# VectorE's attention and router operations in program order, an earlier bias copy, and a kept output product

## Chip, core and metric

The kernel runs on one core of one Trainium2 chip. The metric is the device time of one execution in microseconds (us). Engines: TensorE (PE; its weight loads are listed as PEld), VectorE (DVE), ScalarE (ACT), GpSimd (POOL), SyncE (SP, which only issues DMAs here).

## The reference, cut to what matters

Two layers on x of shape (2, 2048, 256), float32. Layer 0 is a gated linear attention plus a quantised linear layer. Layer 1, which the change touches, is softmax attention plus a mixture of experts chosen by a Sinkhorn router:

```python
xn = _layernorm(x, axis=-1)
# attention: 16 heads of 16; the first 8 look back, the last 8 ahead (ALiBi bias)
scores = jnp.einsum('bhqd,bhkd->bhqk', q, k) * (1.0 / np.sqrt(hd)) + bias[None]
attn = jax.nn.softmax(scores, axis=-1)
out = jnp.einsum('bhqk,bhkd->bhqd', attn, v)
...
return out @ Wf + bf
# router: 20 Sinkhorn iterations on 4096 tokens x 8 experts, two experts for each token
for _ in range(n_iters):
    la = la - jax.scipy.special.logsumexp(la, axis=-1, keepdims=True)
    la = la - jax.scipy.special.logsumexp(la, axis=-2, keepdims=True)
...
_, top_idx = jax.lax.top_k(pi, TOP_K)
...
x = x + _L1_attn_ref(...) + _L1_ffn_ref(...)
```

## The kernel before

The program has three stages in time: layer 0 (to about 437 us), attention with the router in the background (437 to 997 us), and the experts (997 us to the end).

A scheduler in the tile framework sets the order of instructions on each engine. It may bring an instruction forward past others of its engine, as its own estimate of the times says. `tc.keep_in_program_order` pins one instruction: pinned instructions keep the order among themselves in which the program writes them.

**Attention** (`attention`, L1613) goes over tiles: per batch b (2), per direction way (2) and per 256 queries qt (8), so 32 tiles. Way 0 goes from the shortest to the longest tile; way 1 then starts with the shortest again. A tile is cut into units of up to 512 columns for each of four rows of heads. In the main loop each unit does the following:
- `scores` (L1741): products sc into PSUM on PE (L1748), exponentials pt on ACT (L1754).
- `keep_only` (L1759): the first two units of a tile lie on the diagonal; VectorE masks their pt with keepmask (L1766), one unit after their scores.
- `add_up` (L1804): two units later (LATE = 2), the weighted sums o_ps on PE (L1779). The one PSUM buffer of o_ps is used by all tiles, so the first sums of a tile wait until VectorE has copied the last tile's to o_sb (L1812).
- one chore: a finished tile leaves a generator `normalise` (L1696), which does one step in each unit: transposes o_tr (L1705), inv and on on VectorE (L1708, L1712); and for the second tile of a pair also transposes on_tr and the copy onT (L1723, L1725), and two output products f_ps, each added to acc on VectorE (L1731, L1736). After way 1 a DMA writes the finished rows of acc (L1739).
- one step of the router's generator `background` (not in the second and third unit of a tile).

**The router** is `DirectSinkhorn` (L1505) and `Routing.steps` (L1927). Each of 20 iterations has two steps: row sums, their reciprocals and a scaling of pi (L1538, L1516, L1517), column sums sk_c (L1541); then a product sk_ps with a matrix of ones on PE (L1544) and the scaling by columns (L1516 to L1547). Then come ranks (L1949 to L1961), weights (L1966, L1970), the product place_ps (L1978, L1979), upto, place (L1982 on), and the rows of the weights' table. `decide` (L1652) tests whether a general program must run, with the product d_ps (L1675). Once the router is done, POOL scatters the rows to a table (L2089), 64 DMAs, two for each 128 tokens.

**The values' bias**, `value_bias` (L1633), is called at a quarter of the units, which is where batch 0 changes its direction: VectorE spreads bv to bvb (L1637, pinned), PE multiplies it with wf to b_ps (L1641), VectorE adds that to half_bias (L1644, L1645).

Pinned before are the copy bvb and, where an o_sb copy was issued since the last unit, the mask behind it; the other VectorE operations of attention and router are free. PSUM has, beside o_ps, seven buffers "mm" that sc, o_tr, on_tr, f_ps, sk_ps, b_ps, place_ps and d_ps share.

The experts' stage (`Experts`, L2210) multiplies blocks of up to 256 rows: x_ps (transposes of loaded rows xb), h_ps (L2179), y_ps (L2195), and adds the results to the output by indirect DMAs (L2204). Its first pieces also work off what chores are left.

Of the kernel before, what the change touches and what calls it, by code (L numbers as in the profile page):

```python
# [61 lines left out]
P = 128  # L62
# [37 lines left out]
VW = H1 * VC + HR - VC  # L100

# [152 lines left out]
def usual_way(ctx, tc, a, out, c, blocks):  # L254
# [25 lines left out]
    routing = Routing(nc, later, a, c)  # L280
    attention(tc, a, out, acc, la, norms, spans, c, operands, ready, routing, blocks)
# [3 lines left out]
def general_way(ctx, tc, a, out, c):  # L285
# [10 lines left out]
    routing = Routing(nc, later, a, c)  # L296
# [1208 lines left out]
class DirectSinkhorn:  # L1505


    def __init__(self, nc, pool, psum, la, pi, grown, ones_mat):
        self.nc, self.pool, self.psum, self.ones_mat = nc, pool, psum, ones_mat
        self.la, self.pi, self.grown = la, pi, grown  # L1510

    def scale(self, sums, axis):

        nc = self.nc
        by = self.pool.tile([P, sums.shape[1]], F32, tag=f"sk_by{axis}", name="sk_by")
        nc.vector.reciprocal(by, sums)  # L1516
        nc.vector.tensor_tensor(  # L1517
            self.pi, self.pi, by.unsqueeze(axis).to_broadcast([P, NT, NE]), ALU.mult
        )
        most = self.pool.tile([P, 1], F32, tag=f"sk_most{axis}", name="sk_most")  # L1520
        nc.vector.tensor_reduce(most, by, AX.X, ALU.max)
        return most

    def steps(self):


        nc, pool, pi = self.nc, self.pool, self.pi
        rmax = pool.tile([P, NT], F32, tag="sk_r", name="sk_r")
        nc.vector.tensor_reduce(rmax, self.la, AX.X, ALU.max)
        nc.vector.tensor_tensor(  # L1530
# [3 lines left out]
        nc.vector.memset(self.grown, 1.0)  # L1534
        yield
        for _ in range(SINKHORN_ITERS):
            rsum = pool.tile([P, NT], F32, tag="sk_r", name="sk_r")
            nc.vector.tensor_reduce(rsum, pi, AX.X, ALU.add)  # L1538
            most = self.scale(rsum, 2)
            csum = pool.tile([P, NE], F32, tag="sk_c", name="sk_c")  # L1540
            nc.vector.tensor_reduce(csum, pi.rearrange("p t e -> p e t"), AX.X, ALU.add)  # L1541
# [4 lines left out]
            nc.vector.tensor_scalar(most, most, cmost, 1.0, ALU.mult, ALU.max)  # L1546
            nc.vector.tensor_tensor(self.grown, self.grown, most, ALU.mult)  # L1547
# [65 lines left out]
def attention(ctx, tc, a, out, acc, la, norms, spans, c, operands, ready, routing, blocks):  # L1613
# [18 lines left out]

    def value_bias():  # L1633


        tc.keep_in_program_order(
            nc.vector.tensor_copy(ready.bvb, ready.bv.unsqueeze(2).to_broadcast([P, 2, P]))  # L1637
        )
        ps = ps_m.tile([P, E], F32, tag="mm", name="b_ps")
        for e in range(2):  # L1640
            nc.tensor.matmul(  # L1641
                ps, lhsT=ready.bvb[:, e, :], rhs=wf[:, e, :], start=e == 0, stop=e == 1
            )
        nc.vector.tensor_tensor(c.half_bias, c.half_bias, ps, ALU.add)  # L1644
        nc.vector.tensor_scalar(c.half_bias, c.half_bias, 0.5, None, ALU.mult)  # L1645

    def router():
        yield from DirectSinkhorn(nc, p2, ps_m, la, pi, grown, c.ones_mat).steps()
        yield from routing.steps(p2, ps_m, pi)
        yield from decide()  # L1650

    def decide():  # L1652

        high = p2.tile([P, 1], F32, tag="high", name="high")
        nc.vector.tensor_reduce(high, norms[:, 0, :], AX.X, ALU.max)
        least = p2.tile([P, 1], F32, tag="least", name="least")
        entry = p2.tile([P, NT, NE], F32, tag="sk_ex", name="entry")
        nc.vector.tensor_tensor(entry, routing.second, pi, ALU.mult)
        of_token = p2.tile([P, NT], F32, tag="sk_r", name="of_token")
        nc.vector.tensor_reduce(of_token, entry, AX.X, ALU.max)  # L1660
        nc.vector.tensor_reduce(least, of_token, AX.X, ALU.min)
        within = p2.tile([P, 1], F32, tag="within", name="within")
        nc.vector.tensor_scalar(within, least, TINY, None, ALU.is_ge)
        small = p2.tile([P, 1], F32, tag="small", name="small")
        nc.vector.tensor_scalar(small, grown, GROWTH, None, ALU.is_le)
        nc.vector.tensor_tensor(within, within, small, ALU.mult)
        inside = p2.tile([P, NSTRIP * HG * 8], F32, tag="sk_part", name="inside", bufs=1)
        nc.vector.tensor_scalar(
            inside, spans.rearrange("p s h n j -> p (s h n j)"), math.exp(-SPAN), None, ALU.is_ge
        )  # L1670
        nc.vector.tensor_reduce(small, inside, AX.X, ALU.min)
        nc.vector.tensor_tensor(within, within, small, ALU.mult)
# [7 lines left out]
        nc.vector.tensor_copy(row, ps)  # L1680
        both = p2.tile([1, P // 2], F32, tag="dboth", name="dboth")
        nc.vector.tensor_tensor(both, row[:, 0 : P // 2], row[:, P // 2 : P], ALU.mult)
        nc.vector.tensor_scalar(both, both, 0.98 * LIMIT**2, None, ALU.is_le)
        ok = p2.tile([1, 1], F32, tag="dok", name="dok")
        nc.vector.tensor_reduce(ok, both, AX.X, ALU.min)
        nc.vector.tensor_scalar(row[:, P : P + 1], row[:, P : P + 1], float(P), None, ALU.is_equal)
        nc.vector.tensor_tensor(ok, ok, row[:, P : P + 1], ALU.mult)
        nc.vector.tensor_scalar(ok, ok, -1.0, 1.0, ALU.mult, ALU.add)
        nc.vector.tensor_copy(c.general, ok)
        nc.vector.tensor_tensor(ok, ok, routing.over[:, 0:1], ALU.max)  # L1690
        nc.vector.tensor_copy(c.special, ok)
# [4 lines left out]
    def normalise(b, way, qt, o_sb):  # L1696
# [11 lines left out]
        nc.vector.reciprocal(inv, by_head[:, :, :, HD])  # L1708
        for n in range(2):

            at = (1 - n) * 64
            nc.vector.tensor_tensor(  # L1712
# [12 lines left out]
        nc.vector.tensor_copy(onT, ps.rearrange("p n t -> p (n t)"))  # L1725
        yield
        t0 = b * TPB + half * 4
        for n2 in range(2):
# [7 lines left out]
            nc.vector.tensor_tensor(acc[:, ts, :], acc[:, ts, :], ps, ALU.add)  # L1736
# [22 lines left out]
    def keep_only(way, pt, masked, pinned):  # L1759

# [5 lines left out]
        ins = nc.vector.tensor_tensor(  # L1766
# [3 lines left out]
        if pinned:  # L1770
            tc.keep_in_program_order(ins)
# [30 lines left out]
    o_ps, routed, unmasked, copied = None, False, None, False  # L1802

    def add_up():  # L1804
        nonlocal o_ps, copied
# [3 lines left out]
        weighted_sums(step, pieces, pt, o_ps, first, last)  # L1809
        if done:  # L1810
            o_sb = p2.tile([P, 2 * QT], F32, tag="o_sb", name="o_sb")
            nc.vector.tensor_copy(o_sb, o_ps)  # L1812
            copied = True
            chores.append(normalise(*step, o_sb))
            rest.append(True)
            b, way, qt = step
            if qt == (0 if way else N // QT - 1) and b + 1 < B:
                operands.load_values(b + 1, way, values[b, way])
                for g in range(2):
                    operands.load(b + 1, 2 * way + g)  # L1820

# [30 lines left out]
    at = 0  # L1852
    experts = Experts(tc, a, out, c, rooms, blocks)
    ahead = experts.todo[0:2]
    for n, (step, pieces, widths, masked, first, last, done) in enumerate(units):
        b, way, qt = step
        if n == len(units) // 4:
            value_bias()
# [8 lines left out]
        if unmasked:  # L1867
            keep_only(*unmasked, copied)
        unmasked, copied = (way, pt, masked) if masked is not None else None, False
        waiting.append((step, pieces, pt, first, last, done))  # L1870
        if len(waiting) > LATE:
            add_up()
        if rest:
            rest.pop()
        elif chores:
            if next(chores[0], True):
                chores.popleft()
# [8 lines left out]
    if unmasked:  # L1886
        keep_only(*unmasked, copied)
# [4 lines left out]
    for _ in experts.pieces(begun=True):  # L1892
        for _ in range(2):
            if chores and next(chores[0], True):
                chores.popleft()


class Routing:
# [3 lines left out]
    def __init__(self, nc, pool, a, c):  # L1902
        self.nc, self.a, self.c = nc, a, c
# [23 lines left out]
    def steps(self, pool, psum, pi):  # L1927
# [5 lines left out]
        nc = self.nc  # L1933
# [14 lines left out]
        for ts in (slice(0, NT // 2), slice(NT // 2, NT)):  # L1948
            nc.vector.tensor_tensor(beaten[:, ts], other[:, ts], mine[:, ts], ALU.is_gt)  # L1949
            yield  # L1950
            nc.vector.tensor_tensor(equal[:, ts], other[:, ts], mine[:, ts], ALU.is_equal)
            yield
            equal_f = equal[:, ts].rearrange("p t e j -> p t (e j)")
            nc.vector.tensor_tensor(
# [4 lines left out]
            nc.vector.tensor_tensor(beaten[:, ts], beaten[:, ts], equal[:, ts], ALU.add)  # L1959
            yield  # L1960
            nc.vector.tensor_reduce(rank[:, ts], beaten[:, ts], AX.X, ALU.add)  # L1961
            yield
        part = tile_("sk_part", [P, NT, NE], tag="sk_part")
        for r, mark, to in ((0, first, self.weights), (1, second, part)):
            nc.vector.tensor_scalar(mark, rank, float(r), None, ALU.is_equal)
            nc.vector.tensor_tensor(  # L1966
# [3 lines left out]
        nc.vector.tensor_tensor(self.weights, self.weights, part, ALU.add)  # L1970
# [3 lines left out]
        nc.vector.tensor_tensor(both, first, second, ALU.add)  # L1974
# [7 lines left out]
        nc.vector.tensor_copy(upto.rearrange("p t e -> p (t e)"), in_front[:, 1, :])  # L1982
        place = tile_("place", [P, NT, NE], tag="sk_part")
        nc.vector.tensor_tensor(
# [5 lines left out]
        while step < NT:  # L1990
            more = tile_(f"upto{step}", [P, NT, NE], tag="sk_ex")
            nc.vector.tensor_copy(more[:, 0:step, :], upto[:, 0:step, :])
            nc.vector.tensor_tensor(
# [7 lines left out]
        nc.vector.tensor_scalar(number, count, float(BS // 2 - 1), None, ALU.add)  # L2001
        nc.vector.tensor_scalar(number, number, BS.bit_length() - 1, None, ALU.logical_shift_right)
        blocks = tile_("blocks", [P, 2, NE])
        full, half = blocks[:, 0, :], blocks[:, 1, :]
        nc.vector.tensor_copy(full, number)
        in_full = tile_("in_full", [P, NE])
        nc.vector.tensor_scalar(in_full, full, float(BS), None, ALU.mult)
        nc.vector.tensor_tensor(half, count, in_full, ALU.is_gt)
        yield
        end = blocks  # L2010
        for step in (1, 2, 4):
            more = tile_(f"end{step}", [P, 2, NE])
            nc.vector.tensor_copy(more[:, :, 0:step], end[:, :, 0:step])
            nc.vector.tensor_tensor(
# [5 lines left out]
        nc.vector.tensor_tensor(start, end[:, 0, :], full, ALU.subtract)  # L2020
        nc.vector.tensor_scalar(start, start, float(BS), None, ALU.mult)

        away = tile_("away", [P, NE])
        nc.vector.tensor_tensor(away, end[:, 1, :], half, ALU.subtract)
        nc.vector.scalar_tensor_tensor(away, end[:, 0, :], -2.0, away, ALU.mult, ALU.add)
        nc.vector.tensor_scalar(
# [4 lines left out]
        nc.vector.tensor_tensor(place, place, upto, ALU.add)  # L2031
        beyond = tile_("beyond", shape, tag="sk_equal")
        nc.vector.tensor_tensor(
            beyond, place, in_full.unsqueeze(1).to_broadcast(shape), ALU.is_ge
        )
        nc.vector.tensor_tensor(beyond, beyond, away.unsqueeze(1).to_broadcast(shape), ALU.mult)
        yield
        nc.vector.tensor_tensor(place, place, start.unsqueeze(1).to_broadcast(shape), ALU.add)
        nc.vector.tensor_tensor(place, place, beyond, ALU.add)
        yield  # L2040
        for to, mark in zip(self.places, (first, second)):
            own = tile_("own", [P, NT, NE], tag="sk_beaten")
            nc.vector.tensor_tensor(own, place, mark, ALU.mult)
# [374 lines left out]
```

## Time and profile before

| | |
|---|---|
| three runs | 1751.08, 1756.57, 1751.8 us; median 1751.8 |
| profiled execution | 1751.09 us, its span 1749.3 us, granted TensorE clock 0.985 |
| 0 to 437 us | PE busy 397.17, DVE 298.37, ACT 210.24 us |
| 437 to 997.4 us | PE busy 542.70, DVE 225.60, ACT 464.34 us |
| 997.4 us to the end | PE busy 734.15, DVE 165.81, ACT 128.94 us |

Views used: the page's busy shares; windows (busy time of each engine in a stretch, with the clock granted to TensorE as a share of full speed); waits (engine and row, what ended the idle time, total us, times, longest); and the timeline (start, us, engine, line, operation, output<-inputs, shape, and in brackets the idle time just before and what ended it). A wait is put down to the event that came last.

### The profile page before, as it was taken

The numbers are of one execution on the slowest core, as the hardware profiler recorded it, in microseconds if no ns is written. First come the engines' busy times: TensorE is split into PE (matmuls) and PEld (weight loads), VectorE is DVE, ScalarE is ACT, GpSimd is POOL, SyncE is SP. The second block draws the span as 40 slices with busy tenths as digits, with TensorE's granted clock in tenths as the row PEclk, the third lists the DMA queues.
The fourth block names the chain that finished last, engine by engine and source line by source line (L and its number), as shares of the span: only waits on it lengthen the run. The fifth ranks groups of instructions, "written<-read, shape, count | busy, mean of one in ns | idle before, by whom it ended". The sixth has DMA issues, their size and how long they took to land.

```text
span 1749.3 us, 31875 instructions
## 1 busy us (share of the span) xinstructions
PE 1674.0 (96%) x13314; PEld 1298.2 (74%) x13314; DVE 689.8 (39%) x1831; ACT 803.5 (46%) x1590; POOL 394.6 (23%) x350
## 2 busy tenths in 40 slices
PE   7789999999999889999999999999999999999996
PEld 4556766676666656666666788898898888889885
DVE  7888666653665652232232122222222222222221
ACT  4445455554888668888978721111111112111110
POOL 4332221221100004333300112222222222222211
PEclk9999999999999899999999999999999999999998
DMA  9611114114600302622130355566556555556531
GB/s 262 165 37 38 39 51 103 50 50 118 114 2 13 67 20 72 135 70 65 48 125 14 117 204 169 166 219 197 166 171 219 170 180 184 172 180 233 165 86 17
DMA packets 82505, 204.34 MB, mean 117 GB/s; under 512 B 8624, under 2 KB 64304, under 8 KB 71728
## 3 DMA queue, kind: packets, MB, share of 16 engines
q0 software_dynamic: 24944, 138.33, 24.6%
q1 hardware_dynamic: 56304, 62.71, 13.5%
q8 instruction: 107, 1.75, 0.4%
q10 hardware_dynamic: 1104, 1.18, 0.2%
q14 instruction: 46, 0.38, 0.1%
HBM read 152.26 MB, written 49.92 MB: 116 GB/s over the span
## 4 chain that ended last, share of the span: by engine, by line
PE 80%; DVE 12%; ACT 4%; POOL 2%; issue 1%; DMA 1%; SPq 0%; POOLq 0%; DVEq 0%
PE h_ps L2179 27%; PE y_ps L2195 14%; PE sc L1748 11%; PE o_ps L1779 10%; ACT pt L1754 3%; PE y_ps L518 2%; PE vf_ps L518 2%; PE f_ps L1731 2%; DVE pt L1766 2%; PE qk_ps L518 1%; PE vg_ps L518 1%; PE tr L568 1%; PE g_ps L518 1%; PE o_tr L1705 1%; PE q_ps L518 1%
## 5 line engine op out<-in xcount | busy, mean ns | idle before, releaser
L1754 ACT ACTIVATE pt<-sc,shift 128x512 f32<-128x512 f32 (+3 forms) x832 | 463.8, 680 | 96.2 <-PE sc L1748 93.4
L2179 PE MATMUL h_ps<-va,qk 128*128 128x256 f32 (+1 forms) x2368 | 484.3, 365 | 0.0
L2179 PEld LDWEIGHTS h_ps<-va,qk 128*128 128x128 f32 x2368 | 425.4, 190 | 53.3 <-ACT va L2161 0.2
L2184 ACT ACTIVATE sg<-h_ps 128x256 f32<-128x256 f32 (+1 forms) x296 | 109.2, 369 | 593.8 <-PE h_ps L2179 593.8
L1748 PE MATMUL sc<-qk 32*128 32x256 f32 (+6 forms) x3680 | 276.4, 370 | 3.9 <-DVE onT L1725 1.7
L2185 DVE TENSOR_TENSOR larger<-sg,h_ps 128x256 f32<-128x256 f32 (+1 forms) x296 | 119.3, 403 | 355.4 <-ACT sg L2184 355.4
L1748 PEld LDWEIGHTS sc<-qk 32*128 32x128 f32 x3680 | 201.7, 187 | 62.1 <-ACT pt L1754 28.2
L1779 PE MATMUL o_ps<-pt,va 128*32 128x256 f32 (+7 forms) x3680 | 227.4, 350 | 9.0 <-DVE o_sb L1812 8.0
L1779 PEld LDWEIGHTS o_ps<-pt,va 128*32 128x32 f32 x3680 | 121.8, 109 | 87.6 <-issue 28.2
L2204 POOL DMA_INDIRECT out<-va,to x69 | 110.1, 1595 | 214.8 <-DVE larger L2185 85.6
L1766 DVE TENSOR_TENSOR pt<-pt,keepmask 128x1024 f32<-128x1024 f32 x64 | 78.3, 1225 | 187.8 <-ACT pt L1754 187.8
L2195 PE MATMUL y_ps<-qk,larger 128*128 128x256 f32 x560 | 124.3, 379 | 1.0 <-DVE va L2200 1.0
L2195 PE MATMUL y_ps<-larger 128*128 128x256 f32 x544 | 120.4, 379 | 0.0
L2195 PEld LDWEIGHTS y_ps<-qk,larger 128*128 128x128 f32 x560 | 104.8, 190 | 14.8 <-DVE va L2200 1.4
L2089 POOL DMA_INDIRECT table<-rows,place x64 | 70.3, 1099 | 197.1 <-DMA table<-rows,place 134.8
L2200 DVE SCALAR_TENSOR_TENSOR va<-y_ps,wt,half_bias 128x256 f32<-128x256 f32 x69 | 30.4, 479 | 209.6 <-PE y_ps L2195 209.6
L2195 PEld LDWEIGHTS y_ps<-larger 128*128 128x128 f32 x544 | 102.0, 190 | 13.1
L2119 POOL DMA_INDIRECT qk<-in_wgateup,wrow x37 | 36.7, 992 | 292.3 <-PE h_ps L2179 153.2
L518 PE MATMUL vf_ps<-qk,xnT 128*128 128x512 f32 x128 | 58.1, 608 | 0.0
L518 PEld LDWEIGHTS vf_ps<-qk,xnT 128*128 128x128 f32 x128 | 24.1, 194 | 28.8 <-issue 26.7
L1736 DVE TENSOR_TENSOR acc<-acc,f_ps 128x512 f32<-128x512 f32 x32 | 22.0, 687 | 54.3 <-PE f_ps L1731 54.1
L194 POOL TENSOR_TENSOR mx_r<-mx_r,mx_pw 128x512 f32<-128x512 f32 x17 | 22.2, 1307 | 76.3 <-DVE mx_r L193 76.3
(246 smaller groups left out, 1725.4 us busy)
## 6 DMA issues: line engine op xcount, KB each, us to landing
xb<-table SPq DMA_DIRECT2D x32, 265.0 KB
qk<-qk SPq DMA_DIRECT2D x32, 256.0 KB
qk<-qk SPq DMA_DIRECT2D x64, 128.0 KB
table<-spare SPq DMA_DIRECT2D x3, 2120.0 KB
va<-v SPq DMA_DIRECT2D x4, 1208.0 KB
v<-v SPq DMA_DIRECT2D x8, 574.0 KB
normed<-xn SPq DMA_DIRECT2D x8, 512.0 KB
rows<-normed POOLq DMA_DIRECT2D x16, 256.0 KB, 3.4
```

The lines of the kernel that those rows point to most:

```text
L518: tc.keep_in_program_order(nc.tensor.matmul(*args, **kwargs))
L1748: nc.tensor.matmul(scs[r][:, at : at + q1 - q0], lhsT=heads[rows, 1, kb * P : (kb + 1) * P], rhs=heads[rows, 0, qt * QT + q0 : qt * QT + q ...
L1754: nc.scalar.activation(pt[:, r, 0:width], scs[r][:, 0:width], AF.Exp, bias=shift)
L1766: ins = nc.vector.tensor_tensor(part, part, mask[:, 1 - way, :].unsqueeze(1).unsqueeze(1).to_broadcast([P, 4, 2, P]), ALU.min,)
L1779: nc.tensor.matmul(o_ps[r * HR : (r + 1) * HR, to + q0 : to + q1], lhsT=va[:, kb, h * VC : h * VC + HR], rhs=pt[:, r, at : at + q1 - q0], ...
L2089: self.nc.gpsimd.indirect_dma_start(out=self.c.table, in_=rows[:, n, :], in_offset=None, out_offset=bass.IndirectOffsetOnAxis(ap=to[:, 2 * ...
L2119: e.nc.gpsimd.indirect_dma_start(out=w, out_offset=None, in_=e.a[name], in_offset=bass.IndirectOffsetOnAxis(ap=e.c.wrow[:, self.b : self.b ...
L2179: nc.tensor.matmul(ps[:, j, rows], lhsT=self.wgu[:, j, c, f * P : (f + 1) * P], rhs=self.xT[:, c, rows], start=c == 0, stop=c == 1,)
L2184: nc.scalar.activation(sg, ps[:, 0, rows], AF.Silu)
L2185: nc.vector.tensor_tensor(self.hT[:, f, rows], sg, ps[:, 1, rows], ALU.mult)
L2195: nc.tensor.matmul(ps[:, c, :], lhsT=self.hT[:, fc, c * P : (c + 1) * P], rhs=self.wd[:, fc, :], start=fc == 0, stop=fc == NFC - 1,)
L2204: nc.gpsimd.indirect_dma_start(out=out, out_offset=bass.IndirectOffsetOnAxis(ap=self.to[:, c : c + 1], axis=0), in_=y[:, c, :], in_offset= ...
```

## The change

1. A wrapper `InOrder` stands for `nc.vector` in attention and router and pins every operation that it begins. The general program keeps the plain engine.
2. `value_bias` becomes a generator. Its copy bvb is issued four units ahead of its product; the product stays at a quarter of the units.
3. A chore is now a list: the generator, the steps that are left (4 for the second tile of a pair, otherwise 1), and whether it is such a second tile. With the last step the generator is run to its end at once. The last step of a second tile (its second f_ps) is held back until the next tile has left its chore, and is then issued in front of that next tile change's first weighted sums, so between the scores and the sums.

```diff
+class InOrder:
+    def __init__(self, tc, engine):
+        self.tc, self.engine = tc, engine
+    def __getattr__(self, name):
+        begin = getattr(self.engine, name)
+        return lambda *a, **k: self.tc.keep_in_program_order(begin(*a, **k))
...
-    routing = Routing(nc, later, a, c)
-    attention(tc, a, out, acc, la, norms, spans, c, operands, ready, routing, blocks)
+    vector = InOrder(tc, nc.vector)
+    routing = Routing(nc, vector, later, a, c)
+    attention(tc, a, out, acc, la, norms, spans, c, operands, ready, routing, blocks, vector)
...
     def value_bias():
-        tc.keep_in_program_order(
-            nc.vector.tensor_copy(ready.bvb, ready.bv.unsqueeze(2).to_broadcast([P, 2, P]))
-        )
+        vector.tensor_copy(ready.bvb, ready.bv.unsqueeze(2).to_broadcast([P, 2, P]))
+        yield
...
-        nc.vector.tensor_tensor(c.half_bias, c.half_bias, ps, ALU.add)
-        nc.vector.tensor_scalar(c.half_bias, c.half_bias, 0.5, None, ALU.mult)
+        vector.tensor_tensor(c.half_bias, c.half_bias, ps, ALU.add)
+        vector.tensor_scalar(c.half_bias, c.half_bias, 0.5, None, ALU.mult)
+        yield
...
-        if pinned:
-            tc.keep_in_program_order(ins)
...
         if done:
             o_sb = p2.tile([P, 2 * QT], F32, tag="o_sb", name="o_sb")
-            nc.vector.tensor_copy(o_sb, o_ps)
-            copied = True
-            chores.append(normalise(*step, o_sb))
+            vector.tensor_copy(o_sb, o_ps)
+            both = qt % 2 != way
+            chores.append([normalise(*step, o_sb), 4 if both else 1, both])
             rest.append(True)
...
+    def do_chore():
+        chores[0][1] -= 1
+        next(chores[0][0])
+        if not chores[0][1]:
+            for _ in chores.popleft()[0]:
+                pass
...
-        if n == len(units) // 4:
-            value_bias()
+        if n in (len(units) // 4 - 4, len(units) // 4):
+            next(bias)
...
+        spare = chores and chores[0][1] == 1 and len(chores) > 1
         if len(waiting) > LATE:
+            if spare and waiting[0][3]:
+                do_chore()
             add_up()
         if rest:
             rest.pop()
-        elif chores:
-            if next(chores[0], True):
-                chores.popleft()
+        elif chores and (len(chores) > 1 or chores[0][1] != 1 or not chores[0][2]):
+            do_chore()
```

In all other lines of the diff `nc.vector` becomes `vector` in the bodies of `DirectSinkhorn`, `Routing.steps`, `decide`, `normalise` and `keep_only`, with nothing else changed.

## The prediction

> **What bounds the kernel now.** I read the page's busy shares and chain first, then the busy time per 20 us window through the attention stage (437 to 997 us), then TensorE's (PE's) waits in that stage, then the timeline round each long one.
>
> ```profile
> PE 1674.0 (96%) x13314; PEld 1298.2 (74%) x13314; DVE 689.8 (39%) x1831; ACT 803.5 (46%) x1590; POOL 394.6 (23%) x350
> PE 80%; DVE 12%; ACT 4%; POOL 2%; issue 1%; DMA 1%; SPq 0%; POOLq 0%; DVEq 0%
> ```
>
> TensorE sets the end. VectorE (DVE) is 39% busy, so only its order can cost anything, where TensorE waits for it. By windows (window; length; busy us of PE, PEld, DVE, ACT, POOL; clock granted to TensorE; DMA):
>
> ```profile
> 560.00:580.00 20.00, 16.01 (x231) 12.07 (x223) 12.79 (x39) 12.26 (x22) 0.00 (x0) 0.94 0.43 100
> 580.00:600.00 20.00, 18.72 (x204) 12.45 (x206) 16.10 (x26) 12.41 (x25) 1.40 (x3) 0.72 0.54 69
> 640.00:660.00 20.00, 15.59 (x170) 9.68 (x168) 13.87 (x61) 10.52 (x19) 3.50 (x4) 0.83 0.06 23
> 660.00:680.00 20.00, 19.84 (x312) 13.74 (x308) 3.80 (x6) 18.11 (x33) 8.71 (x13) 1.00 0.30 92
> ```
>
> The last is the usual state: 0.16 us idle, clock full. The other three lose 4 us or work at a lowered clock. The waits of PE in the stage name the cause (total, times, longest):
>
> ```profile
> PE o_ps L1779 <- DVE o_sb L1812: 8.0, 20, 2.4
> PE b_ps L1641 <- DVE bvb L1637: 4.0, 1, 4.0
> PE f_ps L1731 <- DVE within L1672: 1.9, 1, 1.9
> PE sc L1748 <- DVE onT L1725: 1.7, 3, 0.6
> PE o_ps L1779 <- DVE pt L1766: 0.9, 1, 0.9
> PE sc L1748 <- DVE place L1984: 0.6, 1, 0.6
> ```
>
> Nearly all of PE's idle time is owed to VectorE, and the timeline shows why: router operations that nobody awaits stand ahead of the one that TensorE needs.
>
> ```profile
> 530.50 0.61 DVE L1541 TENSOR_REDUCE sk_c<-pi 128x8 f32<-128x256 f32 x1
> 531.03 0.68 DVE L1812 COPY o_sb<-o_ps 128x512 f32<-128x512 f32 x1
> ...
> 531.76 1.07 PE L1779 MATMUL o_ps<-pt,va 128*32 128x256 f32 x16 [2.34 <-DVE o_sb L1812]
> ```
>
> ```profile
> 576.77 1.21 DVE L1951 TENSOR_TENSOR sk_equal<-pi 128x1024 bf16<-128x1024 f32 x1
> 577.90 0.15 DVE L1547 TENSOR_TENSOR grown<-grown,sk_most 128x1 f32<-128x1 f32 x1
> 577.97 0.28 DVE L1637 COPY bvb<-bv 128x256 f32<-128x256 f32 x1
> ...
> 578.40 2.04 PE L1641 MATMUL b_ps<-cwf,bvb 128*128 128x256 f32 x4 [3.99 <-DVE bvb L1637]
> ```
>
> The same happens to o_sb at 642.14 (upto, number, place ahead of it) and to onT at 651.92 (mine, row, inside ahead of it).
>
> **What the Trainium skill says.** "TensorE: Matmul & The Clock Gate", Part 1, says that an idle TensorE falls to half clock and needs a busy window of about 3.4 us to come back, and that the window runs free of the program. This trace agrees: after the 3.99 us wait the clock reads 0.50 from 578.4 to 588.3; after 2.38 us (642.9) it reads 0.61 over 4.0 us and after 1.93 us (652.7) 0.56 over 3.9 us, while the 2.34 us wait at 531.8 was followed by full clock. So a wait costs itself, and often half of the next 4 us. "PSUM — Partial Sum Buffer", Engine vs sequencer instructions, says that VectorE's queue is strictly first in, first out: what stands behind a waiting instruction waits too. The rows above show that.
>
> **Part 1: program order on VectorE, what goes.** The diff pins the router and the attention in the order they are written. In the changed order, as built, o_sb again follows its tile's last product and the mask of the next tile's first unit, with no router row between. I price each lost stretch as elapsed time less what the same products take at full clock elsewhere in this trace (eight 256-column score products 1.07, eight weighted sums 1.00, four o_tr 0.59, two f_ps 1.06).
> - A, 529.42 to 531.76: 2.34.
> - B, 574.41 to 594.41 holds b_ps 1.06, three units of scores 2.70, sums 1.00, o_tr 0.59, scores 1.12, sums 0.58, scores 1.07, together 8.12; 20.00 - 8.12 = 11.9. That is 3.99 idle, the rest half clock and a refill, since ScalarE had run dry (10.15 us idle) and two masks stood behind router rows until 587.07.
> - C, 640.50 to 648.11 holds 1.00 + 0.59 + 1.07 + 1.00 = 3.66; lost 3.95, and 0.60 just ahead at 638.76: 4.55.
> - D, 650.81 to 656.57 holds 1.06 + 1.25; lost 3.45.
>
> Together 22.2 us. The early copy bvb (0.28 us, four units, some 9 us, ahead) is part of B: b_ps then waits for nothing. Its DVE time lies beside PE work.
>
> **What program order adds.** VectorE now also stands still where the scheduler used to slip router rows in. I walked the new order with the old durations; behind each such wait stands the row that PE asks for next.
> - First tile: the row-sum half of the Sinkhorn iteration (1.91 from 436.15 to 438.06, in an idle stretch) now follows the second mask, which ended at 441.43. It ends at 443.3, the next mask (ready 442.52) and o_sb move to 445.2, the sums that began at 444.40 wait: 0.85.
> - A product f_ps, then acc (0.69), then a row half (1.85), then sk_ps of the next unit. In the first pair acc ends at 461.92, sk_c at 463.8; sk_ps, whose second f_ps has been taken away, would start at 462.75: 1.1. In the second pair the unit is longer: 0.65. In the other pairs a different half falls there.
> - The short tiles where the direction changes (after b_ps): first, the mask must await four exponentials of 0.6, so o_sb comes 1.1 late, which no reordering removes; in the next tile inv, on and a 1.21 us comparison stand before the mask: 1.2. Together 2.3.
> - upto and place (0.84) before the mask and o_sb at place_ps: 0.7.
> - The decision's 16 rows (about 3.3 by their start-to-start distances) now follow onT of the tile at 692; d_ps, at 695.17 before, waits for within until about 696.1: 1.0.
>
> Together 6.6. None is bounded by a row of its own: below, 2 (half of them hidden by work that I count as late); above, 13 (twice) and three of them long enough to lower the clock, 1.5 each as at D (3.45 - 1.93), so 17.5. I take 6.6.
>
> **Part 2: the product kept for tile changes.** Of the 20 waits on o_sb, 18 are the usual ones: (8.0 - 2.34 - 2.38) / 18 = 0.18 each, because o_sb stands behind a mask that waits for ScalarE. The second f_ps (1.06) of each pair now runs just there, and covers it. Fifteen products move; about half of the waits: 9 x 0.18 = 1.6. Bounds: 0, and 3.3 if all went. The drain of a finished chore without a unit of its own moves one DMA of out some 2 us earlier; it waits in SP's queue for nothing that PE needs.
>
> **What moves with the router.** Its results come later in the program: the first scatter from 650.5 to about 657 on the new clock, place0 being one tile further down. The 64 scatters are a chain of 3.47 us each (650.5 to 872.7), so they end near 879; behind them on POOL stand two weight gathers (874.5 before), on SP the loads of xb (904), and the first use is x_ps, at 989.4 before and some 17 us earlier now. 90 us of cover: nothing. Layer 0 keeps its order, and the experts' stage (997 to the end, PE busy 734.15 of 751.6) keeps its length and starts earlier.
>
> **Sum.** -22.2 - 1.6 + 6.6 = -17.2. The profiled execution took 1751.09, span 1749.3 with 1.8 round it: span 1732.1, time 1733.9. The median shown is 1751.8, 0.7 above that execution: 1734.6.
>
> **Rivals.**
> - Half gain. More waits of the new kind than I found, at the upper bound: -22.2 - 0 + 12 to 17.5, a gain of 5 to 10, some 1744. For it: 40 Sinkhorn halves stand in the first 130 us, where VectorE is 62% busy (80.56 of 130.00). Against: half a unit (1 us or more) of slack in most units that I walked.
> - More gain. The new waits mostly vanish and the usual o_sb waits too: -22.2 - 3.3 + 2 = -23.5, 1728. Against: the first short tile's wait is in the data flow.
> - Slower. One mechanism: the chain sk_c, sk_ps, reciprocal, row half becomes the bound of the first 130 us, as VectorE may no longer bring a half forward. Twenty row halves; from (22.2 + 1.6 - 4.85 of the other new waits) / 20 = 0.95 us each it eats the gain. With 1.25 us each the time is 1758. Against: without f_ps in its unit a row half has over 4 us until its sk_ps.
> - The change doesn't do what it says: the pinned rows stay behind others. The order as built excludes it: no router row stands before o_sb or bvb's user any more.
>
> **Chances.** Forecast (1730 to 1740) 0.68; half gain (1740 to 1747) 0.19; more gain (under 1730) 0.08; slower 0.05. The range 1729 to 1743 leaves out the slower case, half of the half-gain case and some of the more-gain one. A measurement of this kernel can tell some 0.3% (5.3 us) from no change: faster, under 1746.5, 0.91; same 0.05; slower 0.04.
>
> **What would show it.** In the profile after: no wait of PE on VectorE above 1.5 us in the attention stage; bvb gone from the list; the clock at 1.00 from 440 to the stage's end; the first h_ps near 980 instead of 997.4; waits on o_sb of 0.16 at only every second tile change; new entries of about 1 us for sk_ps <- sk_c and d_ps <- within. Wrong it would be if sk_ps waits dozens of times, if the clock still falls near 580, or if the experts' stage begins with a wait on xb.

## The result, and the profile after

| | before | after |
|---|---|---|
| median of 4 runs | 1752.9 us | 1731.91 us |
| range | 1751.08 to 1756.57 | 1730.19 to 1733.55 |
| profiled execution, its span | 1751.09, 1749.3 | 1733.55, 1731.7 |
| first score product to first h_ps | 434.86 to 997.40 = 562.54 | 435.09 to 977.58 = 542.49 |
| first h_ps to the h_ps behind the second x_ps | 18.98 | 21.90 |

The ratio of the times is 0.9878, 95% interval 0.9864 to 0.9893. The forecast was 1734.6, with a range of 1729 to 1743. The profiled execution before was the fastest of its four and the one after the slowest of its four, so this pair differs by 17.5 us where the medians differ by 21.0.

The page of the kernel after, busy shares and chain:

```profile
PE 1668.3 (96%) x13314; PEld 1297.7 (75%) x13314; DVE 696.3 (40%) x1831; ACT 802.3 (46%) x1590; POOL 389.6 (22%) x350
PE 80%; DVE 9%; issue 6%; POOL 2%; ACT 2%; DMA 1%; SPq 0%; POOLq 0%; DVEq 0%
```

TensorE's trace has the same 13314 products. VectorE's share of the chain falls from 12% to 9%. TensorE's waits from 440 to 985 us, after (total, times, longest):

```profile
PE y_ps L2221 <- DMA qk<-in_wdown,wrow: 3.0, 1, 3.0
PE o_ps L1793 <- DVE o_sb L111: 2.8, 11, 0.6
PE d_ps L1693 <- DVE within L111: 0.8, 1, 0.8
PE sk_ps L1557 <- DVE sk_c L111: 0.5, 1, 0.5
```

(L111 is the wrapper, which now records every pinned operation of VectorE.) The 4.0 on bvb, the 1.9 on within, the 1.7 on onT, the 0.9 on pt and the 0.6 on place are gone, and no wait on VectorE is longer than 0.8. At the top stands a wait that was not there before, on a DMA. The same windows as before, of the kernel after (window; length; busy us of PE, PEld, DVE, ACT, POOL; clock; DMA):

```profile
560.00:580.00 20.00, 20.00 (x302) 15.05 (x291) 12.39 (x40) 17.16 (x32) 0.00 (x0) 1.00 0.28 48
580.00:600.00 20.00, 19.01 (x270) 12.12 (x263) 14.87 (x24) 16.16 (x30) 0.00 (x0) 1.00 0.71 122
640.00:660.00 20.00, 20.00 (x305) 13.66 (x301) 12.13 (x41) 17.60 (x33) 0.65 (x1) 1.00 0.08 28
660.00:680.00 20.00, 19.07 (x285) 13.11 (x281) 9.16 (x30) 17.27 (x31) 7.74 (x10) 1.00 0.19 61
```

Where the clock read 0.72 and 0.83, it reads 1.00, and ScalarE has 16 to 18 us of work where it had 10 to 12. The new wait stands where the experts begin. Timeline after:

```profile
975.62 0.94 POOL L2145 DMA_INDIRECT qk<-in_wdown,wrow  x1 [1.23 <-PE sc L1765]
...
977.58 3.72 PE L2205 MATMUL h_ps<-va,qk 128*128 128x256 f32 x16
...
984.72 1.10 PE L2221 MATMUL y_ps<-qk,larger 128*128 128x256 f32 x4 [2.98 <-DMA qk<-in_wdown,wrow]
985.65 0.60 PE L1740 MATMUL on_tr<-ident,on 128*128 128x128 f32 x4
```

and of the kernel before:

```profile
995.45 0.94 POOL L2119 DMA_INDIRECT qk<-in_wdown,wrow  x1 [1.23 <-PE sc L1748]
...
1015.07 0.60 PE L2157 MATMUL x_ps<-ident,xb 128*128 128x128 f32 x4
1015.51 1.03 PE L2195 MATMUL y_ps<-qk,larger 128*128 128x256 f32 x4
```

In both the gather of the down-weights starts as soon as the last scores have released its buffer, 2 us before the first h_ps. Before, the first y_ps came 20 us later. After, the scheduler has brought it forward in front of on_tr, some 9 us behind the gather, and TensorE waits. So the attention stage gains 20.05 us, and the experts' start gives back 2.92; with +0.23 before the stage and -0.7 after it this is the span's -17.6.

Beside the waits of d_ps on within and of sk_ps on sk_c in the list, something was paid at the two short tiles where the direction changes. Timeline after:

```profile
578.77 1.90 PE L1765 MATMUL sc<-qk 32*128 32x256 f32 x16
581.04 1.07 PE L1793 MATMUL o_ps<-pt,va 128*32 128x256 f32 x16 [0.37 <-DVE o_sb L111]
...
584.30 1.53 PE L1765 MATMUL sc<-qk 32*128 32x256 f32 x18
586.44 1.07 PE L1793 MATMUL o_ps<-pt,va 128*32 128x256 f32 x16 [0.62 <-DVE o_sb L111]
```

The waits in brackets are 0.99, but the score products ahead of them are stretched too: 16 of them take 1.07 at full pace. From 578.77 to 581.04 is 2.27, so 1.20 lost; from 584.30 to 586.44 is 2.14 where 18 need 1.20, so 0.94. The list of waits shows less than half of these 2.1 us: TensorE counts as busy through a group of products even where they start further apart than usual.

### The profile page after: what moved, and what is told of

It reads as the page before. It is cut to its first block, busy times and chain, and to the rows that moved or that the text cites. A ratio compares the mean times of both kernels' runs of the same rounds, so it can differ in the third digit from the quotient of the medians.

```text
span 1731.7 us, 31881 instructions
## 1 busy us (share of the span) xinstructions
PE 1668.3 (96%) x13314; PEld 1297.7 (75%) x13314; DVE 696.3 (40%) x1831; ACT 802.3 (46%) x1590; POOL 389.6 (22%) x350
## 3 DMA queue, kind: packets, MB, share of 16 engines
q8 instruction: 107, 1.75, 0.4%
## 4 chain that ended last, share of the span: by engine, by line
PE 80%; DVE 9%; issue 6%; POOL 2%; ACT 2%; DMA 1%; SPq 0%; POOLq 0%; DVEq 0%
PE h_ps L2205 27%; PE y_ps L2221 14%; PE sc L1765 10%; PE o_ps L1793 9%; PE y_ps L530 3%; PE vf_ps L530 2%; PE tr L580 2%; PE f_ps L1748 2%; PE g_ps L530 2%; PE vg_ps L530 1%; PE qk_ps L530 1%; PE q_ps L530 1%; PE o_ds_ps L530 1%; ACT pt L1771 1%; PE o_tr L1722 1%
## 5 line engine op out<-in xcount | busy, mean ns | idle before, releaser
L111 DVE TENSOR_TENSOR pt<-pt,keepmask 128x1024 f32<-128x1024 f32 x64 | 78.4, 1225 | 190.9 <-ACT pt L1771 190.9
L2115 POOL DMA_INDIRECT table<-rows,place x64 | 65.8, 1028 | 176.6 <-DMA table<-rows,place 135.0
L205 POOL TENSOR_TENSOR mx_r<-mx_r,mx_pw 128x512 f32<-128x512 f32 x17 | 22.2, 1307 | 76.4 <-DVE mx_r L204 76.4
L806 ACT ACTIVATE kept<-state,to_next 128x128 f32<-128x128 f32 x56 | 20.9, 397 | 36.6 <-DVE state L841 36.6
```

The lines of the kernel that those rows point to most:

```text
L111: return lambda *a, **k: self.tc.keep_in_program_order(begin(*a, **k))
L2115: self.nc.gpsimd.indirect_dma_start(out=self.c.table, in_=rows[:, n, :], in_offset=None, out_offset=bass.IndirectOffsetOnAxis(ap=to[:, 2 * ...
```

## Experiments

**Theory**: the gain comes from VectorE's order. Router operations that nobody awaits stood ahead of attention operations that TensorE awaits; all three parts of the change share in undoing this, and the early y_ps takes some 3 us back. **Rivals**: it is enough to order attention's own operations; the late bvb alone was the cause; the kept product alone; the new waits on sk_c come from the moved product.

All medians in us. "Stage" is from the first score product to the first h_ps in the one profile of that run. The first four ran on one chip, the next four on another (without the changed kernel), and the last four in pairs, each beside the kernel before. The stage of the changed kernel took 540.99 to 542.49 in its three profiles, and 542.36 to 543.13 in the four of the y_ kernels, which differ only behind it. So a difference of under 2 us between two stages says little, and one of a few us between two medians not much more: the six runs of after_again spread from 1731.15 to 1736.85. There the lists of waits carry the argument.

| run | median | ratio to before, interval | stage |
|---|---|---|---|
| after_again | 1733.05 | 0.9886 (0.9865 to 0.9906) | 542.05 |
| y_held | 1729.77 | 0.9864 (0.9843 to 0.9885) | 542.50 |
| late_bias | 1736.74 | 0.9903 (0.9883 to 0.9922) | 544.77 |
| no_kept | 1735.03 | 0.9894 (0.9875 to 0.9914) | 543.40 |
| router_free | 1742.29 | 0.9946 (0.9927 to 0.9965) | 553.80 |
| pins_only | 1736.82 | 0.9907 (0.9885 to 0.9928) | 546.42 |
| bias_only | 1748.48 | 0.9973 (0.9963 to 0.9983) | 558.61 |
| kept_only | 1749.75 | 0.9980 (0.9969 to 0.9991) | 559.02 |
| y_one | 1728.84 | 0.9860 (0.9840 to 0.9881) | 542.86 |
| y_held_2 | 1732.09 | 0.9876 (0.9855 to 0.9898) | 543.13 |
| y_one_2 | 1729.69 | 0.9862 (0.9841 to 0.9883) | 542.36 |
| after_third | 1733.10 | 0.9876 (0.9854 to 0.9898) | 540.99 |

### The changed kernel again

> The changed kernel itself, as the measure for the three kernels beside it. All theories: span about 1730 to 1732, time 1730 to 1734. If the half clock at the start of attention (about 2 us in the first profile) is a matter of where the clock's window falls, this profile may show the clock at full there and a span some 2 us shorter; if the new order causes it, it is there again.

1733.05, with the wait of y_ps on the DMA 3.0 again. The stage's start differed from the first profile. In the first, the clock had fallen:

```profile
435.00:440.00 5.00, 4.52 (x44) 4.12 (x46) 1.87 (x4) 3.89 (x9) 4.06 (x4) 0.75 0.81 243
440.00:445.00 5.00, 5.00 (x59) 2.71 (x55) 4.33 (x8) 2.93 (x7) 5.00 (x2) 0.57 0.98 282
```

In after_again it stayed full, and a wait stood there which the slow clock had covered:

```profile
443.22 1.07 PE L1793 MATMUL o_ps<-pt,va 128*32 128x256 f32 x16 [0.72 <-DVE o_sb L111]
```

From the first score product to the first o_tr it is 10.54 us in the kernel before, 12.70 in the first profile after and 11.20 in this one. So the changed kernel runs without the half clock too, and whether the change makes it likelier isn't shown: 5 of the 11 profiles of versions with pinned attention have it there, and none of the three of versions without. The 0.72 is the work of the change, and was priced at 0.85.

### Holding the first y_ps back

```diff
+    def begin_rows(self, n):
+        ps = self.e.rooms("y_ps", self.n, [P, NC * E]).rearrange("p (c d) -> p c d", c=NC)
+        self.ps = ps, n
+        for fc in range(n):
+            self.e.tc.keep_in_program_order(nc.tensor.matmul(
+                ps[:, 0, :], lhsT=self.hT[:, fc, 0:P], rhs=self.wd[:, fc, :],
+                start=fc == 0, stop=False,
+            ))
...
             if n:
                 todo[n - 1].add_rows()
+            else:
+                block.begin_rows(2)
```

(h_ps and the other y_ps are pinned in the same way; add_rows goes on behind what is begun.)

> The changed kernel with h_ps and y_ps of the experts pinned, and the first y_ps product put after the second x_ps, where the kernel before has it. Theory 1 (the 2.98 us wait of y_ps for the weights' DMA was put there by the scheduler, which moved y_ps ahead of on_tr): the wait goes, nothing takes its place, 2.9 us less than the changed kernel beside it. Rival (the weights are late anyway, now that attention ends earlier): the wait comes back at the later y_ps, no gain.

The wait on the DMA goes; from the first h_ps to the first y_ps TensorE waits only here (timeline of y_held):

```profile
980.99 0.63 PE L1740 MATMUL on_tr<-ident,on 128*128 128x128 f32 x4 [1.27 <-DVE on L111]
...
993.98 1.03 PE L2221 MATMUL y_ps<-qk,larger 128*128 128x256 f32 x4
```

From the first h_ps to the h_ps behind the second x_ps it takes 19.29, against 23.56 in after_again. These 4.3 are more than the wait, because in after_again half clock followed it (timeline of after_again):

```profile
982.18 1.87 PE L2221 MATMUL y_ps<-qk,larger 128*128 128x256 f32 x4 [2.95 <-DMA qk<-in_wdown,wrow]
983.85 1.06 PE L1740 MATMUL on_tr<-ident,on 128*128 128x128 f32 x4
```

In the first profile after the same products took 1.10 and 0.60. The span is 2.5 below after_again's, since the rest of the two executions differs by 1.8 the other way, and the median is 3.3 lower. That nothing takes the wait's place was wrong: on_tr waits 1.27 for VectorE's inv and on. In the changed kernel that time lay inside the wait for the DMA; the kernel before had 0.96 of it.

### Filling the wait of on_tr

y_held, with one step of the left chores for each of the experts' first pieces:

```diff
     for _ in experts.pieces(begun=True):
-        for _ in range(2):
-            if chores:
-                do_chore()
+        if chores:
+            do_chore()
```

> The kernel y_held (the first y_ps products behind the second x_ps, in program order) with one step of the left chores for each of the experts' first pieces instead of two, so that eight h_ps products of the next piece (1.9 us) stand between o_tr and on_tr. Theory: the wait of on_tr on VectorE's on (1.27 in y_held, 0.97 in the kernel before) is a wait for a chain of 2 us behind o_tr (inv, on) that no other PE work covers; with the products between it goes, and the time falls by about 1.2 against y_held on the same chip. Rival: another wait takes its place (f_ps on the copy onT, or the last y_ps rows on the later end of the output's first rows): 0 to 0.5 gained, or lost.

> The kernel y_held once more, beside y_one on the same chip: 1728 to 1732, its first y_ps without a wait on a DMA, on_tr waiting about 1.3 us.

The products of the next piece now stand between; they take 3.6 us, where 1.9 was expected (timeline of y_one):

```profile
981.39 0.60 PE L1722 MATMUL o_tr<-ident,o_sb 128*128 128x128 f32 x4
981.83 3.62 PE L2205 MATMUL h_ps<-va,qk 128*128 128x256 f32 x16
985.29 0.60 PE L1740 MATMUL on_tr<-ident,on 128*128 128x128 f32 x4
...
994.80 1.03 PE L2220 MATMUL y_ps<-qk,larger 128*128 128x256 f32 x4
```

From the first h_ps to the h_ps behind the second x_ps it takes 17.82, against 19.28 in y_held_2: 1.46 saved, and no wait takes its place. The median is 3.3 lower, more than this explains; the ranges of 5 and 4 runs overlap (1727.5 to 1732.57 and 1730.56 to 1733.21). The comparison with the changed kernel itself was made on one chip:

> The kernel y_one once more, now beside the changed kernel on one chip. Theory: it saves the wait of the first y_ps on its weights' DMA (3.0) and the wait of on_tr (1.0 to 1.3), so about 4 us below the changed kernel, 1727 to 1731. Rival: part of the saving is given back where the experts' stage ends, since its total of transfers is unchanged: 0 to 2 us below.

> The changed kernel, for the comparison with y_one on one chip: 1730 to 1735, the wait of the first y_ps 3.0 us.

1729.69 (1726.95 to 1731.14) against 1733.10 (1729.75 to 1733.92): 3.4 less where 4 were expected. In the profiles the start of the experts is 5.8 shorter (17.82 against 23.64), as half clock followed the wait in after_third too. This version is below both kernels; 3.4 us are 0.2%, less than one such comparison can tell surely, but the two waits are absent from both of its profiles.

### The bias copy at its old place

```diff
-        if n in (len(units) // 4 - 4, len(units) // 4):
+        if n == len(units) // 4:
+            next(bias)
             next(bias)
```

> The changed kernel with the bias copy again beside its product. Theory 1 (program order alone removes stretch B; the early copy is a trifle): b_ps waits about 0.5 us, since only half a Sinkhorn iteration stands before the copy; time 0.5 to 1 us above the changed kernel. Rival (the early copy is what removes B): a wait of about 4 us at b_ps with the clock at half after it, 4 to 12 us above.

It cost 3.7 in the median against after_again and 2.3 in the stage against the first profile after (both begin at half clock). That is more than the theory's 0.5 to 1 and less than the rival's 4 to 12, and it isn't a wait on bvb (timeline of late_bias):

```profile
576.19 1.10 PE L1657 MATMUL b_ps<-cwf,bvb 128*128 128x256 f32 x4
578.44 6.19 ACT L1771 ACTIVATE pt<-sc,shift 128x512 f32<-128x512 f32 x12 [4.42 <-PE sc L1765]
579.18 3.22 PE L1765 MATMUL sc<-qk 32*128 32x128 f32 x26 [0.60 <-ACT pt L1771]
```

and the same row of ScalarE in the kernel after:

```profile
576.71 6.20 ACT L1771 ACTIVATE pt<-sc,shift 128x512 f32<-128x512 f32 x12 [2.71 <-PE sc L1765]
```

b_ps waits for nothing, because the scheduler put 22 weighted sums ahead of b_ps and of the next scores, which the kernel after has behind the first of these scores. ScalarE runs dry for 4.42 instead of 2.71, and these 1.71 come out at TensorE: the sums that start 145.95 us into the stage after start 147.70 into it here. What else the median lost wasn't found. The early copy is worth something through the order of products that comes with it.

### Without the kept product

```diff
-            chores.append([normalise(*step, o_sb), 4 if both else 1, both])
+            chores.append([normalise(*step, o_sb), 4 if both else 1, False])
...
-        spare = chores and chores[0][1] == 1 and len(chores) > 1
+        spare = False
```

> The changed kernel without the kept product: the second f_ps follows the first one unit later. Theory 1: waits on o_sb rise from 2.8 us to about 4, time 1.5 us more. Rival (the kept product costs as much as it covers, because sk_ps then comes sooner than sk_c): no difference, and the wait of sk_ps for sk_c goes.

Waits of TensorE in no_kept:

```profile
PE o_ps L1793 <- DVE o_sb L111: 5.6, 22, 0.7
...
PE sk_ps L1557 <- DVE sk_c L111: 0.6, 1, 0.6
```

Twenty-two waits on o_sb instead of the 12 of after_again, 2.0 us more. The median rises by as much, though at a size that the runs alone would not show. The wait on sk_c stays, so it doesn't come from the moved product.

### The router free, attention in order

The changed kernel with the plain engine handed to Routing, DirectSinkhorn and decide:

```diff
-    routing = Routing(nc, vector, later, a, c)
+    routing = Routing(nc, nc.vector, later, a, c)
...
-        yield from DirectSinkhorn(nc, vector, p2, ps_m, la, pi, grown, c.ones_mat).steps()
+        yield from DirectSinkhorn(nc, nc.vector, p2, ps_m, la, pi, grown, c.ones_mat).steps()
```

> The changed kernel, but the router's operations on VectorE (the Sinkhorn iterations, the ranks and places, the decision) stand free again, so that the scheduler may place them ahead of others; attention's own operations, the early copy and the kept product stay as changed. Theory 1, the prediction's: the lost stretches A to D come from router rows placed ahead of an attention row that TensorE awaits. Pinning attention's rows among themselves does not stop this, so several of the long waits return (o_sb, onT or the mask behind router rows), TensorE waits 5 us or more in the stage on VectorE beyond the changed kernel's usual ones, the clock falls under 1.00 in at least one window between 500 and 700 us: 1737 to 1745. Rival: it is enough that attention's own rows keep their order among themselves (mask, o_sb, inv, on, onT, acc); then the list of waits stays as in the changed kernel and the time is 1731 to 1734.

The long waits are back (waits of router_free, the stage):

```profile
PE o_ps L1794 <- DVE o_sb L111: 8.3, 13, 2.4
PE on_tr L1741 <- DVE over L2097: 1.7, 1, 1.7
PE f_ps L1749 <- DVE onT L111: 1.5, 1, 1.5
PE f_ps L1749 <- DVE row L2093: 0.5, 1, 0.5
```

and one of them, at 580.21, reads on VectorE so:

```profile
576.60 0.68 DVE L1986 TENSOR_TENSOR sk_beaten<-sk_beaten,sk_equal 128x1024 bf16<-128x1024 bf16 x1
577.20 1.22 DVE L1976 TENSOR_TENSOR sk_beaten<-pi 128x1024 bf16<-128x1024 f32 x1
578.34 1.22 DVE L111 TENSOR_TENSOR pt<-pt,keepmask 128x1024 f32<-128x1024 f32 x1
579.47 0.68 DVE L111 COPY o_sb<-o_ps 128x512 f32<-128x512 f32 x1
```

Mask and copy keep their order between themselves, and the router's comparisons stand ahead of both. The stage is 11.3 longer than in the first profile after (both begin at half clock), and the median is 9.2 above after_again's, which ran on another chip; the intervals of the two ratios don't meet. The rival falls: ordering attention alone leaves about half of the gain behind.

### Each part by itself

Program order alone is the changed kernel with the edits of late_bias and no_kept together.

> The changed kernel without the kept product and with the values' bias copied at its old place: program order on VectorE alone. Theory 1: the parts add. Taking the kept product away cost 2.0 us and taking the early copy away 3.7, against the changed kernel of the same chip; together 1737 to 1740, with some 20 to 22 waits on o_sb, the wait of the first y_ps on its weights' DMA of about 3.0 us still there, and a dry ScalarE near 578. Rival: the two losses are one and the same (the later bias shifts the tiles so that the kept product has nothing to cover), then 1735 to 1737.

1736.82 lies in the range of the rival (1735 to 1737) and 0.2 below that of the theory, so the medians don't settle whether the losses add. The stages fit a sum: no_kept against after_again 1.35, late_bias against the first after 2.28, together 3.63; pins_only against the first after 3.93. With the spread of single stages, and with half clock in pins_only from 580 on (0.83 over 10 us) that neither of the two others has, this is no proof. Both marks do stand side by side: 20 waits on o_sb, and ScalarE dry for 4.42 before the short tile's exponentials.

The early copy alone, on the kernel before:

```diff
-        if n == len(units) // 4:
-            value_bias()
+        if n in (len(units) // 4 - 4, len(units) // 4):
+            next(bias)
```

> The kernel before, with the copy bvb alone issued four units earlier; everything else as before. Theory 1: the router rows ahead of o_sb and onT remain, so A, C and D (2.34, 4.55 and 3.45 us) or stretches like them stay; of B (11.9) the wait of 3.99 goes, but the masks and sums behind router rows stay, so that no more than half of B is won: 1745 to 1751 beside a kernel before of about 1752. Rival: the late copy alone was the cause of all of B, then 1739 to 1743. Second rival: other rows merely take the copy's place (the list of waits keeps its sum): no gain, 1751 to 1754. The first y_ps stays behind x_ps, without a wait on a DMA.

Waits of bias_only:

```profile
PE o_ps L1781 <- DVE o_sb L1814: 10.9, 22, 2.4
PE f_ps L1733 <- DVE within L1674: 1.9, 1, 1.9
...
PE f_ps L1733 <- DVE onT L1727: 1.5, 1, 1.5
```

The wait of 4.0 is gone, and from 560 to 600 us the clock reads 0.96 where it read 0.83. But o_sb waits 1.80 at 579 and 1.15 at 587 and f_ps 1.53 for onT at 592, all new and all behind router rows: TensorE is busy for 35.31 of these 40 us, against 34.72 before and 39.01 after. The stage gains 3.9 of the 11.9 of B; the bvb wait was the largest sign of the fault, not its cause.

The kept product alone, on the kernel before (the edits of part 3 of the change):

> The kernel before, with the kept product alone. Theory 1: it covers the usual waits of o_sb behind the mask, so their number falls from 18 to about half, worth 1.6 us (the changed kernel lost 2.0 without it), with A to D as they were: 1749.5 to 1752 beside a kernel before of about 1752. Rival: with the router's rows free the scheduler reshuffles them around the moved product, the long waits stand elsewhere, and the time goes either way by more than 3 us; the list of waits would then show other long entries than b_ps, f_ps and the two of o_sb.

Waits of kept_only:

```profile
PE o_ps L1779 <- DVE o_sb L1812: 6.6, 11, 2.4
PE b_ps L1641 <- DVE bvb L1637: 4.0, 1, 4.0
PE f_ps L1731 <- DVE within L1672: 1.9, 1, 1.9
```

The usual waits on o_sb fall by 1.4, and the three of 0.56 of sc on onT (618.94, 762.30 and 896.52 before) are gone: 1.7 more. Together 3.1 of the 3.5 by which the stage is shorter. The long ones stand where they were. By stage the parts alone give 3.9, 3.5 and 16.1, together 23.6, of which 20.1 to 21.6 are left when all are made: they partly remove the same thing. Program order is by far the largest part, the more so as the stage of pins_only began at half clock.

## Why the prediction was right, and where it was not

- **Which waits go (22.2 us).** Held. All four stretches are gone and the clock reads 1.00 there, and router_free shows the cause that was named. The sum closes on the stage of after_again: -22.2 for A to D, -1.4 for usual waits on o_sb, -1.7 for the waits on onT, and +4.3 of new ones (next point) make -21.0; measured were -20.5 (-20.1 to -21.6 in three profiles). One of the signs named did not come in the first profile, the clock at 1.00 from 440 on: it read 0.57 from 440 to 445.
- **What program order adds (6.6).** Over-sized. The start took 0.66 (0.85 was said), the short tiles 2.1 with their stretched scores (2.3 said) and d_ps 0.8 to 1.0 (1.0 said). But sk_ps waited once, 0.5, where two waits of 1.75 together were said, and nothing waited behind place_ps (0.7 said). Some 4.3 in all. The waits that came are of the kinds that were named; their sum was mis-sized. The walk was done with the durations of the old order and took no profit of the rows that moved out of the way; that this is the reason was not tested.
- **The kept product (1.6).** The usual o_sb waits fell from 3.3 to 1.8, so this term held. The waits of sc on onT were left out of the sum: 1.7 that the list showed as three entries. In pins_only they are gone too, so that program order alone removes them as well.
- **The experts' stage "keeps its length".** This step failed. Its start is 2.9 longer in the first profile after, 4.6 and 4.7 in the other two, since the first y_ps goes ahead of on_tr on TensorE and waits for its weights, and in those two half clock followed. The first y_ps stands there in every version that pins attention's operations, router_free included, and in neither bias_only nor kept_only; why the scheduler does it is not shown. The edits touch neither line; only TensorE's order after the change tells it, and the prediction followed the order of VectorE and the queues of POOL and SP. It asked whether xb is late, not whether the gather of the down-weights is.
- **The sum.** -17.2 said, -17.6 measured in the span. This is closer than the steps deserve, and so in part luck: new waits 2.3 too large and 1.7 of onT waits missed on the one side, 2.9 for y_ps missed on the other, and the half clock at the first profile's start (1.5) against it. The medians fell by more, 21.0, and the one after lies 2.7 below the forecast.
- **The early copy "is part of B".** As an addend its own value could not be read, and the experiments show why: 3.9 alone, 2.3 beside the other parts (hardly more than single stages spread), and by no wait of its own in the latter.
- **Rivals.** The chain of sk_c did not become the bound (one wait of 0.5), and the 12 to 17.5 of new waits in "half gain" did not come. "More gain" named part of what came, new waits that vanish: 4.3 were left, between its 2 and the 6.6 of the forecast. Its 1728 was not reached even with the first y_ps held back (y_held: 1729.77 and 1732.09).

## What to carry to other kernels

When a background task shares an engine with work that the bounding engine awaits, pin both, in one program order: pinning the awaited operations among themselves leaves the background ahead of them, and removing the largest single wait lets the next background row take its place. When a change lets a scheduler re-order, compare the new order on the bounding engine to the stage's end and check the transfers that each moved product waits for; the costs that come back sit outside the edited lines. In a list of waits, add to a wait the stretch of the group ahead of it, since a group whose products start too far apart still counts as busy.

## What the hardware showed that was not expected

A little idling can bring the half clock, or not, in the same code. In the first profile after, TensorE worked at full clock up to 434 us and then idled 0.97 us and 0.39 us round the stage's first score products; the clock read 0.73 in the microsecond from 437 and 0.50 from 438. With the same two waits after_again kept 1.00 there. Behind the wait of the first y_ps it was the other way round: 2.98 us in the first profile left the clock at 1.00, 2.95 in after_again brought 0.50 from 983 to 985, and the start of the experts took 1.7 longer (23.56 against 21.90). The Trainium skill, "TensorE: Matmul & The Clock Gate", Part 1, says that the window runs free, so that the cost varies from run to run, which agrees; its idle window of about 3.4 us for the fall does not, as the idle time that the timeline lists ahead of these two falls is 1.4 us in two pieces and 2.95 us.

The attention stage also begins at different times in one and the same kernel, 435.09, 433.02 and 435.23 in its three profiles, so that differences of 2 us between single spans say nothing before the stages are laid side by side.

The mean clock of whole executions differs as well, and the time with it. Beside the experiments the kernel before ran 73 times: with a mean clock of 0.985 or more it took 1748.79 to 1753.12, with 0.982 or less 1753.79 to 1757.44. So no single profile shows what a wait costs on average.
